# A delta-rule attention layer and its feed-forward layer: the loads for the next unit called at the beginning of a slot

## The chip, the cores and the metric

The kernel runs on one core of a Trainium2 chip. The metric is device time in microseconds (us). Before the change it is 4428.87 us, the median of three runs (4426.77 to 4429.70).

## The reference, cut to what matters

The input x has 4 sequences of 1024 positions with 256 features. The first half is a gated delta-rule attention with 16 key heads and 32 value heads of 128 features each; positions go in chunks of 64. All of it is in 32-bit floats.

```python
mixed = silu(conv4(x @ W_qkv.T))          # causal, 4 taps
q, k, v = split(mixed); q, k = l2n(q), l2n(k)
beta = sigmoid(b);  g = -exp(A_log) * softplus(a + dt_bias);  gc = cumsum(g) in a chunk
decay = exp(gc_i - gc_j) * tril
A  = -((k*beta) @ k.T * decay) * strict
Tm = inverse(eye - A)                     # 64 x 64 for each chunk and head
u  = Tm @ (v*beta);  kcd = Tm @ (k*beta*exp(gc))
# in order of the chunks, with a state S (128 x 128) for each sequence and head:
attn  = (q @ k.T) * decay
v_new = u - kcd @ S
out   = (q*exp(gc)) @ S + attn @ v_new
S     = S * exp(g_last) + (k * exp(g_last - gc)).T @ v_new
y = (out * rsqrt(mean(out**2) + eps) * norm_w * silu(z)) @ W_out.T
```

Then x = x + layernorm(y), and a feed-forward layer (688 inner features, weights taken from a table of 16 values) with a layer norm and a residual of its own.

## The kernel before

**Units, blocks, groups.** The 32 value heads are worked in eight groups of four. A group goes through the 64 chunk positions in 32 tiles of 128 rows: a tile, together with the group's four heads, is a *unit*, so there are 256 units. Within a unit two sequences lie one above the other (64 rows each). Eight units make a *block* (`Super`, 32 in all). The place of a unit in its block, 0 to 7, is u.

**What is made for a unit ahead of its step.** `channel` projects and convolves (matmuls pp, L422; four taps on ACT and DVE, L436 and L439; Silu, L443) and stores q and k in DRAM as qkd (L445). `scores` loads decay rows (dc, L522), multiplies them on POOL (L529 to L536) with the products kkq (L545) and stores the lower triangle lT and the attention scores aT to DRAM (L561). `invert` loads lT for a whole block as lb (L569), inverts all 32 x 32 diagonal pieces at once on DVE by 31 rank-one steps (rank and v, L579 and L580), and stores them as vd (L583). `build` makes the off-diagonal piece of each inverse with two rounds of small matmuls (m1 L611 and m2 L625) out of the loads mt (L599) and pad (L601 and L606), and stores it as nd (L634).

**What the change moves.** `expand(k, u)` (L636 on) lays these out for one unit, with nine DMAs on SP's queue: four ue<-vd (L643) and two ue<-nd (L649) put the inverse pieces at their places in the zeroed tile ue, two ae<-atd (L651) do the same with the scores in ae, and one qku<-qkd (L654) fetches q and k. There are three buffers of ue and of ae, and two of qku.

**The step of a unit.** `step(k, u)` is a generator, and each `yield` ends a part: N0 transposes v into x0; N1 is the product of k and q with the state (pkqs, L683, reads qku); N2 is px (L703, reads ue), the transposes pk (L714, read qku), and the decay of the state on POOL (L720); O3 is po (L703, reads ae) and core (L727). Then J makes squares (L732), and O4 is the state's update (pu, L740, and L747). N parts run in the unit's own slot, O parts in the next one. `project_out` comes five units later (Z, T, U: pz L142, L781 to L785, pto L789, pout L796); it loads the sum ac so far (L775) and stores it again (acc_d, L802).

**The order around the change.** The loop at L871 goes through slots s; slot s runs the step of unit s. A slot's list in `SLOTS` gives the order of the parts by hand, and on TensorE, ScalarE, VectorE and GpSimd instructions stay in that order (`manual_schedule(engines=COMPUTE)`). SP, which issues all DMAs, is not among these: a planner puts its queue in order when the program is built. It takes the transfers that it believes ready, and of several that are ready the one that the program calls for first. On the chip SP then goes through that queue strictly one by one, and waits where a transfer isn't ready yet. The list for the slot that ends in the step of place 7, in which the loads of the next block's place 0 are called for, begins `v1 A b O3 ...`: v1 calls for the lb loads, b for the store of nd. The slot ahead of that one begins with `b`, which calls for the loads mt and pad.

Of the kernel before, what the change touches and what calls it, by code (L numbers as in the profile page):

```python
# [63 lines left out]
def delta_net_ffn_kernel(  # L64
# [243 lines left out]
    with ExitStack() as main:  # L308
# [327 lines left out]
        def expand(k, u):  # L636

            at = (supers.index(k) * SB + u) % NZ
            ue, ae = (zeroed[name][at] for name in ("ue", "ae"))
            for q in range(4):  # L640
                rows = slice(q * BS, (q + 1) * BS)
                src = k.vd[q * BS + u * HG : q * BS + (u + 1) * HG, :, :]
                nc.sync.dma_start(ue[rows, :, rows], src.rearrange("h c i -> c h i"))  # L643
            for ab in range(2):
                a0 = ab * C
                lo, hi = slice(a0, a0 + BS), slice(a0 + BS, a0 + C)
                hb, w = divmod(u * HG, NQ)
                q = slice((2 * ab + hb) * BS, (2 * ab + hb + 1) * BS)
                nc.sync.dma_start(ue[lo, :, hi], k.nd[q, w : w + HG, :])  # L649
                half = slice(a0, a0 + C)  # L650
                nc.sync.dma_start(ae[half, :, half], k.atd[half, u, :, :])  # L651
            k.exp[u] = ue, ae
            qku = sc.tile([P, MG, 2, 2, C], F32, tag="qku", name="qku", bufs=2)
            nc.sync.dma_start(qku.rearrange("p m j a t -> p m j (a t)"), k.qkd[u])  # L654
            k.qku[u] = qku
# [93 lines left out]
        def rms(k, blk):  # L749
            us = slice(4 * blk, 4 * blk + 4)  # L750
            rr = w2.tile([P, 4, HG], F32, tag="rr", name="rr", bufs=3)
            eq = w2.tile([P, 4, MG], F32, tag="eq", name="eq")
            V.tensor_scalar_mul(eq, k.n2[:, us, :, 1], RMS_EPS * D)
            V.scalar_tensor_tensor(
                rr.rearrange("p c (m h) -> p (c m) h", h=2),
                k.ms[:, us, :].rearrange("p c (m h) -> p (c m) h", h=2),
                1.0 / D,
                bc(eq.rearrange("p c m -> p (c m)").unsqueeze(2), [P, 4 * MG, 2]),
                ALU.mult,
                ALU.add,  # L760
            )
            V.reciprocal(rr, rr)
            yield
            A.activation(rr, rr, AF.Sqrt)
            k.rr[blk] = rr
            yield

        def project_out(k, u):

            end = k.last and u == SB - 1 and k.g + 1 < NG  # L770
            wzs = w_z[k.g]
            ti = k.t0 + u
            ac = sc.tile([P, HID], F32, tag="ac", name="ac", bufs=3)
            if k.g:
                nc.sync.dma_start(ac, acc_d[ti])  # L775
            pz = bank("pz")
            by_rows(pz, lambda kc: wzs[:, kc, :], ti)
            if end:
                load_z(k.g + 1)
            zs = t4("zs")  # L780
            A.activation(zs, as4(pz), AF.Silu)  # L781
            yield 1
            G_.tensor_tensor(zs, zs, bc(k.rr[u // 4][:, u % 4, :].unsqueeze(2), h4), ALU.mult)  # L783
            yield 1
            G_.tensor_tensor(zs, zs, k.cores.pop(u), ALU.mult)  # L785
            yield
            pt = bank("pto")
            for h in range(HG):
                T_.transpose(as4(pt)[:, h, :], zs[:, h, :], ident)  # L789
            oT = t4("oT")  # L790
            A.copy(oT, as4(pt))  # L791
            yield
            wo = w_o[k.g]
            pp = bank("pout")
            for h in range(HG):
                T_.matmul(pp[:, :HID], lhsT=oT[:, h, :], rhs=wo[:, h, :], start=h == 0, stop=h == HG - 1)  # L796
            yield 1
            if k.g == 0:
                V.tensor_copy(ac, pp[:, :HID])
            else:  # L800
                V.tensor_add(ac, ac, pp[:, :HID])  # L801
            nc.sync.dma_start(acc_d[ti], ac)  # L802
            if end:
                load_o(k.g + 1)

        def drain(*gens):
            for gen in gens:
                for _ in gen:
                    pass
# [4 lines left out]
        def resume(gen):  # L814
            nonlocal count
            wait = next(gen, None)
            if wait:
                heappush(due, (place + wait, count, gen))
                count += 1

        def go(gen):

            nonlocal place
            late = [entry for entry in due if entry[2] is gen]
            while late:
                due.remove(late[0])
                heapify(due)
                resume(gen)
                late = [entry for entry in due if entry[2] is gen]
            if gen is not None:  # L830
                resume(gen)
            place += 1
            while due and due[0][0] <= place:
                resume(heappop(due)[2])
# [7 lines left out]
        def work(kind, n, *args):  # L842

            if not 0 <= n < len(supers):
                return None
            key = (kind, n, *args)
            if key not in started:
                started[key] = kind(supers[n], *args)
            return started[key]
# [19 lines left out]
        units = [(k, u) for k in supers for u in range(SB)]  # L869
        with tc.manual_schedule(engines=COMPUTE):  # L870
            for s in range(-LQ, len(units)):  # L871
                n, i = divmod(s, SB)
                nq, iq = divmod(s + LQ, SB)
                nv, iv = divmod(s + LV, SB)
                gens = {}
                newer = step(*units[s]) if s >= 0 else None
                for c in "01234":
                    gens["N" + c], gens["O" + c] = newer, older
                gens["J"] = older
                gens["T"] = gens["U"] = gated  # L880
                gated = project_out(*units[s - OUT_LAG]) if s >= OUT_LAG else None
                gens["Z"] = gated
                if 0 <= nv < len(supers):
                    gens["A"] = channel(supers[nv], iv // 4, 2 * MG + iv % 4, 2)
                if nq < len(supers):
                    gens["B"] = channel(supers[nq], iq // 4, iq % 4, 1)
                inv = work(invert, nq - 1 if iq >= 4 else nq - 2)
                made = work(build, nq - 2)

                root = [work(rms, *divmod(s // 4 - 1, 2))] + ([work(roots, n + 1)] if i == 4 else [])  # L890
                for name in SLOTS[iq].split():
                    c = name[0]
                    if c == "v":
                        for _ in range(int(name[1:]) if inv else 0):
                            next(inv, None)
                        continue
                    block = 2 * nq + iq // 4 - (iq % 4 != 2 or c == "s")
                    if c in "rq":
                        for gen in filter(None, root[: 1 if c == "r" else 2]):
                            resume(gen)  # L900
                        continue
                    if c == "n":
                        gen = work(norms, *divmod(block, 2))
                    elif c == "s":
                        gen = work(scores, *divmod(block, 2))
                    elif c == "b":
                        gen = made
                    else:
                        gen = gens.get(name)
                    go(gen)  # L910
                    if name == "O4":
                        next(pieces, None)
                if inv and iq == 2:
                    drain(inv)
                older = newer
                if 0 <= s + 1 < len(units):
                    expand(*units[s + 1])
            drain(older)
            drain(rms(supers[-1], 1))
            drain(*(gen for _, _, gen in sorted(due)))  # L920
            drain(gated)
            for unit in units[len(units) - OUT_LAG :]:
                drain(project_out(*unit))
            drain(pieces)
# [112 lines left out]
```

## Time and profile before

| | |
|---|---|
| median of 3 runs | 4428.87 us |
| the profiled execution | 4427.16 us |
| its span, first to last instruction | 4425.5 us |
| mean granted TensorE clock | 0.971 |
| instructions in the span | 79446 |
| DMA moved | 492.71 MB, 111 GB/s in the mean |

Read from the page: the chain that ended last is 58% TensorE, 24% DVE, 6% ScalarE and 2% DMA. Up to about 280 us the first blocks are prepared, from there to about 4010 us the slots run, about 14.7 us each in the mean, and the feed-forward layer fills the rest. In the rows of DMA issues, the median time from issue to landing is 2.2 us for ue<-vd, 1.9 us for ue<-nd, 2.6 us for ae<-atd and 3.0 us for qku<-qkd. In the groups by line, "out<-in" are the names of the tiles written and read, and "idle before <-releaser" is who ended the wait.

### The profile page before, as it was taken

To read this page: it belongs to the slowest core of one execution; us is meant where nothing else is said; L and a number is where in the kernel's file an instruction comes from. 1 tells how busy PE (TensorE), PEld (TensorE's weight loads), DVE (VectorE), ACT (ScalarE), POOL (GpSimd) and SP (SyncE) were. 2 spreads that over 40 slices of the span, in tenths; PEclk is the share of its full clock that TensorE was granted. 3 is DMA by queue.
4 is the path that set the end of the run, shared out by engine and by line. 5 is a ranking of instruction groups with operands and counts; after the bars stand their busy time and mean duration, and the time that the engine had idled before them with its cause. 6 is when DMAs were issued, how large, how long until landed. Compare 5 with 4: busy or idle time off the path is not lost.

```text
span 4425.5 us, 79446 instructions
## 1 busy us (share of the span) xinstructions
PE 4007.4 (91%) x26664; PEld 2866.6 (65%) x26664; DVE 3510.1 (79%) x6641; ACT 2646.0 (60%) x6573; POOL 2070.6 (47%) x1752
## 2 busy tenths in 40 slices
PE   3679999999999999999999999999999999996888
PEld 2456666676767766666667676676766766673444
DVE  4788888888888898888888888889888888861442
ACT  2456666666666666666666666666666666662111
POOL 2545555655555555554455545555453334332221
PEclk7899999999999999999999999999999999997999
DMA  3444444444444444444444444444444444432110
GB/s 91 118 112 110 111 118 120 127 121 118 126 136 126 119 118 127 119 118 125 130 128 120 117 126 135 125 116 118 123 123 117 123 126 120 101 83 71 37 35 19
DMA packets 1052419, 492.71 MB, mean 111 GB/s; under 512 B 729824, under 2 KB 951152, under 8 KB 1052016
## 3 DMA queue, kind: packets, MB, share of 16 engines
q1 hardware_dynamic: 1052016, 487.64, 41.8%
q8 instruction: 216, 3.54, 0.3%
q14 instruction: 187, 1.53, 0.1%
HBM read 267.66 MB, written 219.69 MB: 110 GB/s over the span
## 4 chain that ended last, share of the span: by engine, by line
PE 58%; DVE 24%; issue 6%; ACT 6%; POOL 3%; DMA 2%; SPq 0%; DVEq 0%; POOLq 0%; ACTq 0%
PE pp L422 13%; DVE cv L439 8%; PE pout L796 7%; PE pz L142 7%; PE pkqs L683 7%; PE px L703 4%; DVE rank L579 4%; PE pu L740 3%; PE po L703 3%; PE pgu L959 3%; PE py L971 2%; PE kkq L545 2%; DVE v L580 2%; PE pto L789 1%; DVE core L727 1%
## 5 line engine op out<-in xcount | busy, mean ns | idle before, releaser
L439 DVE SCALAR_TENSOR_TENSOR cv<-pp,cw,cv 128x512 f32<-128x512 f32 x1536 | 1148.8, 748 | 353.3 <-ACT cv L436 323.7
L783 POOL TENSOR_TENSOR zs<-zs,rr 128x512 f32<-128x512 f32 x256 | 266.4, 1041 | 1578.8 <-ACT zs L781 1569.8
L436 ACT ACTIVATE cv<-pp,cw 128x512 f32<-128x512 f32 x512 | 350.6, 685 | 488.0 <-PE pp L422 487.9
L580 DVE TENSOR_TENSOR v<-v,rank 128x31 f32<-128x31 f32 (+15 forms) x992 | 555.7, 560 | 34.3 <-DVE rank L579 0.3
L422 PE MATMUL pp<-xnT,wq 128*128 128x262 f32 x2048 | 530.1, 401 | 41.9 <-DVE cv L439 32.6
L796 PE MATMUL pout<-wo,oT 128*128 128x256 f32 x2048 | 510.2, 394 | 7.8 <-ACT oT L791 7.8
L422 PEld LDWEIGHTS pp<-xnT,wq 128*128 128x128 f32 x2048 | 372.0, 191 | 214.5 <-issue 56.2
L422 PE MATMUL pp<-xnT,wv 128*128 128x262 f32 x2048 | 503.8, 387 | 5.5 <-DVE cv L439 5.5
L142 PE MATMUL pz<-wzs,xnT 128*64 128x512 f32 x2048 | 488.4, 598 | 4.7 <-DVE ac L801 3.8
L579 DVE TENSOR_TENSOR rank<-v,lb 128x31 f32<-128x31 f32 (+15 forms) x992 | 467.1, 471 | 27.3 <-DMA lb<-ltd 19.6
L683 PE MATMUL pkqs<-S,qku 128*64 128x256 f32 x3840 | 477.5, 387 | 4.7 <-DVE core L727 3.3
L720 POOL TENSOR_TENSOR S<-S,dkm 128x1024 f32<-128x1024 f32 x224 | 436.3, 1948 | 26.6 <-PE pkqs L683 16.1
L703 PE MATMUL px<-x,ue 128*128 128x128 f32 x2048 | 291.9, 286 | 159.5 <-issue 106.9
L703 PEld LDWEIGHTS px<-x,ue 128*128 128x128 f32 x2048 | 263.3, 194 | 260.0 <-issue 150.2
L422 PEld LDWEIGHTS pp<-xnT,wv 128*128 128x128 f32 x2048 | 382.0, 190 | 73.6 <-issue 12.8
L796 PEld LDWEIGHTS pout<-wo,oT 128*128 128x128 f32 x2048 | 386.6, 199 | 55.6 <-ACT oT L791 9.7
L683 PEld LDWEIGHTS pkqs<-S,qku 128*64 128x64 f32 x3840 | 248.7, 136 | 203.0 <-issue 51.0
L732 ACT ACTIVATE junk<-core 128x128 f32<-128x128 f32 x1024 | 318.7, 311 | 66.7 <-DVE core L727 38.4
L785 POOL TENSOR_TENSOR zs<-zs,core 128x512 f32<-128x512 f32 x256 | 328.5, 1283 | 20.1
L708 ACT ACTIVATE xs<-px 128x512 f32<-128x512 f32 x256 | 154.6, 604 | 234.3 <-PE px L703 234.3
L740 PE MATMUL pu<-yg,kt 64*128 64x256 f32 x1920 | 272.2, 402 | 14.2 <-DVE cv L439 13.1
L300 POOL TENSOR_SCALAR lt<-lx,lutb 128x344 f32<-128x344 int32 (+2 forms) x210 | 276.7, 1317 | 16.8
(166 smaller groups left out, 7067.8 us busy)
## 6 DMA issues: line engine op xcount, KB each, us to landing
qkd<-qk SPq DMA_DIRECT2D x256, 256.0 KB, 2.5
qku<-qkd SPq DMA_DIRECT2D x256, 256.0 KB, 3.0
dc<-rows_d SPq DMA_DIRECT2D x256, 128.0 KB, 3.6
ltd<-lT SPq DMA_DIRECT2D x128, 256.0 KB, 2.4
atd<-aT SPq DMA_DIRECT2D x128, 256.0 KB, 2.7
ae<-atd SPq DMA_DIRECT2D x512, 64.0 KB, 2.6
acc_d<-ac SPq DMA_DIRECT2D x256, 128.0 KB, 2.2
ac<-acc_d SPq DMA_DIRECT2D x224, 128.0 KB, 2.5
```

Source lines behind the costliest of these rows:

```text
L142: T_.matmul(ps[ab * C : (ab + 1) * C, :], lhsT=xnT[:, kc, 2 * p + ab, H + n * C : H + (n + 1) * C], rhs=rhs(kc), start=kc == 0, stop=kc == ...
L422: T_.matmul(ps[:, 2 * p : 2 * p + 2, : H + BT], lhsT=wt[:, kc, :], rhs=xnT[:, kc, 2 * p : 2 * p + 2, c0 : c0 + H + BT], start=kc == 0, sto ...
L436: A.activation(cv, ps[:, :, H : H + BT], AF.Copy, scale=cw[:, ch, H : H + 1])
L439: V.scalar_tensor_tensor(cv, ps[:, :, i : i + BT], cw[:, ch, i : i + 1], cv, ALU.mult, ALU.add)
L579: V.tensor_tensor(t, bc(v[:, 0 : j + 1, j : j + 1], sh), bc(lb[:, j : j + 1, j + 1 :], sh), ALU.mult)
L580: V.tensor_tensor(v[:, 0 : j + 1, j + 1 :], v[:, 0 : j + 1, j + 1 :], t, ALU.subtract)
L683: T_.matmul(as4(ps)[ab * C : (ab + 1) * C, two, :], lhsT=qk[:, m, j, ab, :], rhs=S_[:, ab, two, :], start=True, stop=True,)
L703: T_.matmul(as4(ps)[:, h, :], lhsT=w[:, h, :], rhs=src[:, h, :], start=True, stop=True)
L720: G_.tensor_tensor(flat, flat, bc(decay, [P, 2 * HG, P]), ALU.mult)
L740: T_.matmul(as4(pu[:, ab])[:, two, :], lhsT=kt[half, m, :], rhs=yg[half, two, :], start=True, stop=True)
L785: G_.tensor_tensor(zs, zs, k.cores.pop(u), ALU.mult)
L796: T_.matmul(pp[:, :HID], lhsT=oT[:, h, :], rhs=wo[:, h, :], start=h == 0, stop=h == HG - 1)
```

## The change

`expand` for the unit of the next slot was the last thing that a slot did. Now it is called ahead of the slot's list when the next unit is at place 1 to 7 of its block, and right after part O4 when it is at place 0, whose inverse's last piece is stored in that same slot. Nothing that is computed changes, and `expand` itself doesn't.

```diff
                 root = [work(rms, *divmod(s // 4 - 1, 2))] + ([work(roots, n + 1)] if i == 4 else [])
+
+                ahead = units[s + 1] if 0 <= s + 1 < len(units) else None
+                if ahead and ahead[1]:
+                    expand(*ahead)
                 for name in SLOTS[iq].split():
...
                     go(gen)
                     if name == "O4":
                         next(pieces, None)
+                        if ahead and not ahead[1]:
+                            expand(*ahead)
                 if inv and iq == 2:
                     drain(inv)
                 older = newer
-                if 0 <= s + 1 < len(units):
-                    expand(*units[s + 1])
```

## The prediction

> **What bounds the kernel now.** I read the page first, for the bound. (The columns of its first row: busy us, share of the span, number of instructions.)
>
> ```profile
> span 4425.5 us, 79446 instructions
> PE 4007.4 (91%) x26664; PEld 2866.6 (65%) x26664; DVE 3510.1 (79%) x6641; ACT 2646.0 (60%) x6573; POOL 2070.6 (47%) x1752
> PE   3679999999999999999999999999999999996888
> DMA  3444444444444444444444444444444444432110
> ```
>
> From the third slice to about the 36th, TensorE is busy nine tenths of the time or more, and the 16 DMA engines under half of it. The busy times by stretch agree: 948.32 us of TensorE in the 1000 us from 1000 to 2000. What is left of TensorE's idle time between 280 and 4010 us I took from the trace as gaps over 0.4 us: 187 us, of which 157 stand before px (L703), where they end with the last DVE step of x0 (L694). TensorE and DVE bound the loop.
>
> The change moves only DMA issues, so the next question is who waits for the tiles that they fill. Of the answers for the tiles ue (inverses), qku (q and k) and ae (scores), in this order, the part on who waited for it (us, times):
>
> ```profile
> who waited for it (us, times):
>   ACT xs L708: 234.3, 210
>   POOL S L720: 10.6, 1
>   DVE rank L579: 2.0, 2
> ```
> ```profile
>   POOL S L720: 16.1, 2
>   POOL wo L370: 14.8, 3
>   ACT qs L695: 1.7, 3
>   DVE x L694: 1.2, 1
> ```
> ```profile
>   DVE core L727: 75.9, 68
>   DVE lT L555: 1.2, 1
> ```
>
> No row says PE px, pkqs or po: these are waits for matmuls that read the tiles, and three (10.6, 2.0, 1.2 us) that are put down to a load on the same queue while the waiting line does not read it. So I measured each margin in the trace, as the start of a unit's matmul less the landing of its last load. From unit 1 on the smallest is 11.5 us for px after ue, 14.9 us for po after ae and 8.8 us for px after qku (q and k are read first by pkqs, some 6 us before px); the medians are 30.8, 33.0 and 23.1 us. Unit 0 has 4.2 us for ue and still no wait.
>
> Why so early, if the call stands at the end of the slot ahead? The timeline of SP, around slot 118 (its px starts at 2019.89, the po of unit 117, which opens the slot on TensorE, at 2010.63):
>
> ```profile
> 2007.55 0.58 SPq L651 DMA_DIRECT2D ae<-atd  x1
> 2008.23 0.55 SPq L654 DMA_DIRECT2D qku<-qkd  x1
> 2008.88 1.46 SPq L522 DMA_DIRECT2D dc<-rows_d  x1
> ...
> 2021.28 0.33 SPq L569 DMA_DIRECT2D lb<-ltd  x1
> 2024.10 0.33 SPq L802 DMA_DIRECT2D acc_d<-ac  x1
> 2025.11 0.37 SPq L445 DMA_DIRECT2D qkd<-qk  x1
> 2025.53 1.81 SPq L569 DMA_DIRECT2D lb<-ltd  x3
> 2027.57 1.11 SPq L634 DMA_DIRECT2D nd<-nb  x1
> 2028.72 1.39 SPq L643 DMA_DIRECT2D ue<-vd  x3
> ```
>
> The first two rows are the last loads of unit 119, which slot 118 calls for at its end: they are out before slot 118 begins. SP is not among the engines whose order is written by hand. Its queue stands in an order that the planner chose when it believed each transfer ready, and the place of the call is only a rank among transfers that are ready together. I counted this over the run: all nine loads of unit s+1 are issued before the px of unit s in every slot that I counted (units 16 to 239), and for places 2 to 7 in a block of eight mostly (57 to 100% by place) before slot s has begun. For places 0 and 1 (the place of a unit in its block of eight) they reach into the slot.
>
> **The change, part by part.** Removed: 256 calls at the end of a slot. Added: the same calls, 224 of them ahead of the slot's list and 32 (for a unit at place 0 of its block) after its O4. No compute instruction is added or moved, and their order stays. Each call issues nine transfers, 2304 in all: four ue<-vd, two ue<-nd, two ae<-atd, one qku<-qkd. By the medians of their rows one call holds SP for 4 x 0.430 + 2 x 0.432 + 2 x 0.586 + 0.433 = 4.19 us, before and after. So the sum on the path is: added work 0; stall removed from TensorE 0, since it never waited for these loads.
>
> What can move is the transfers of the same slot that were issued ahead of an expand and are now ranked behind it, by at most 4.19 us each. I took their cover from landing to first reader:
> - ac<-acc_d (L775): at least 21.8 us until L801. In 26 of the 28 blocks that have it, it stands ahead of all loads of the units at places 0 and 1; now it may come after those of place 1. Cost 0.
> - dc<-rows_d (L522): at least 8.3 us until the POOL step L529. In the slot that calls for place 4's loads it now ranks behind them. 8.3 - 4.2 leaves 4.1 us. Cost 0; if that cover were gone, POOL, at 47%, would be late with the scores.
> - pad<-vd from L606: at least 9.4 us until the matmuls L625; mt<-ltd: at least 61 us. Both are issued by build in the slot that calls for place 7's loads, and rank behind these now. Cost 0.
> - pad<-vd from L601: only 0.24 to 3.8 us until the matmuls L611, most often about 3. But it waits for a store of this same slot (L593, issued at 2012.48 once ACT's copy is done), and the loads of unit 119 are out at 2008.8 already. Cost 0.
> - lb<-ltd (L569): the tight one. The inversion's first step L579 waits for it on DVE:
>
> ```profile
>   DMA lb<-ltd: 19.6, 16
> ```
> One of these waits, 6.6 us, is at the start; the other 15 make 13.0 us. In the rows above lb stands ahead of unit 120's loads, and the call for place 0, even after O4, stays behind lb in program order (lb is called for at the first step of the same slot). Cost 0.
>
> A call made earlier might also put a waiting transfer at SP's head. The largest row of SP's own waits says how much of that there is already:
>
> ```profile
> SPq L643 <- PE pk L714: 507.0, 102, 8.1
> ```
> Here SP stands at a first ue<-vd until an older unit's matmuls have let its buffer go, up to 8.1 us, with everything else queued behind. The Trainium skill ("Perfetto Trace Analysis", DMA Instruction — HWDGE) has the semaphore wait on the issuing sequencer, ahead of the descriptors, since the DMA engines themselves don't wait. That speaks against an earlier call: by the rule, a slot whose expand stands first could hold its stores and loads for up to 8.1 us more. The row shows that these waits come from the planner's idea of when the buffer is free, since they exist although the call stands at the slot's end. The buffers are three for ue and ae and two for qku, and are let go one to two slots ahead of either place, so neither place makes a new wait. By the rule, with 32 lb loads held 8.1 us, the sum is up to +259 us; by the row it is 0. I take 0, as all nine loads precede px of the slot today. The opposite rule ("DMA: Bandwidth & Descriptors", Rules for kernel authors: issue the DMA early, wait on its semaphore late) would promise a gain; with 8.8 us of smallest margin there is nothing to collect.
>
> The lower bound of the unknown: a regrouped queue may happen to send the three last lb loads ahead of the qkd store that they now follow (2025.11 above), and that could remove at most the 13.0 us of DVE waits. The upper bound is priced in the slower rival.
>
> **The rivals.**
> *Forecast, no change that can be measured:* the queue's order changes within its slack. Profiled execution 4427.16 us (span 4425.5 and 1.7 around it) + 0 = 4427.2; the median of the runs shown stands 1.7 us above that, so 4429 us, with 5 us either side for a fraction of a microsecond here and there in 32 blocks. Chance 0.72.
>
> *Faster:* lb passes the store, the 13.0 us of DVE waits go, and DVE is what TensorE's px waits for. Against it: the largest of these waits does not reach TensorE. With 1.63 us of it (at 594 us) the eight slots from px of unit 15 to unit 23 take 598.94 - 477.75 = 121.19 us; in the same phase of the next group without such a wait (units 47 to 55) 1077.19 - 955.90 = 121.29. It would need the full 13 us, and gives 4416; a part gives 4420 and less is in the forecast. Chance 0.11.
>
> *Slower:* the regrouped nine loads fall in front of the lb loads (or of the ltd store that they read) at the turn of a block, 32 times. Price: up to 4.19 us each, less the 1.6 us of lateness that the comparison above shows to be free. So it decides from 1.6 us on, about four loads put in front; all nine cost 4.19 - 1.6 = 2.6 us x 32 = 83 us (4512), and six of them 6 x 0.47 - 1.6 = 1.2 us x 32 = 38 us (4467). The rows above speak against it: lb is ranked ahead of place 0's loads, and place 7's are long out. For it speaks only that lb's own margin is nil. Chance 0.17, most of it near the low end.
>
> That the change doesn't do what it says is in effect the forecast: the place of the call doesn't set the time of the issue.
>
> **How the numbers follow.** About 0.2%, 8.9 us, is what a measurement of this kernel can tell from no change. Same 0.72, faster 0.11, slower 0.17, as the cases. The forecast's own range is 4424 to 4434; with 8 in 10 wanted it is reached to the faster case's nearer part and the slower one's low end: 4419 to 4441. The predicted time is the forecast's, 4429.
>
> **What would show it.** Right, if the order of TensorE, DVE, ACT and POOL is as before, px still has ue some 30 us ahead in the median, and in the timeline of SP the loads of a unit stand closer together, with dc and ac behind them. L775 and L522 should then land later at no cost, and the row lb<-ltd stay near 19.6 us in total. Wrong, if a row "PE px <- DMA ue" or "PE m <- DMA pad" appears, if the lb row grows past some 50 us (32 x 1.6), or if the 507.0 us of SP's waits at L643 grow and the qkd or ltd stores behind them come late.

## The result: no change that can be measured

| | before | after |
|---|---|---|
| median of 12 runs each | 4431.07 us | 4433.44 us |
| ratio, 95% interval | | 1.0005 (0.9996 to 1.0014) |
| the same measured once more (e1_again) | 4430.23 us | 4429.42 us |
| ratio, 95% interval | | 1.0001 (0.9993 to 1.0009) |
| span of the profiled execution | 4425.5 us | 4432.7 us, and 4425.9 us in e1_again |

Both intervals hold 1 and end inside the 0.2% that the prediction named. The two profiled spans of the same changed kernel, 4432.7 and 4425.9 us, show how much of a single span's difference is the execution's own. It is not waiting: between the first px of the first unit and that of the last, TensorE is idle for 201.4 us in the one and 200.8 in the other, against 202.6 before the change. It is the granted clock: 0.968 in the mean in the one and 0.970 in the other, with 4021.3 and 4009.9 us of TensorE's busy time for the same matmuls (the last section says where the clock is lost). The prediction was 4429 us, 4419 to 4441.

The page of the changed kernel, first its span, busy times and the 40 slices of TensorE:

```profile
span 4432.7 us, 79363 instructions
PE 4021.3 (91%) x26664; PEld 2876.3 (65%) x26664; DVE 3514.5 (79%) x6641; ACT 2646.0 (60%) x6573; POOL 2069.1 (47%) x1752
PE   3679999999999999999999999999999999995888
```

On TensorE, DVE, ACT and POOL the counts of instructions are those of before, and instruction by instruction none has another place in its engine's order. On SP 1649 of 4478 transfers have. Counted in places of the queue, 425 of the 1024 ue<-vd come earlier (up to 16 places), as do 271 of the 512 ue<-nd, 321 of the 512 ae<-atd and 120 of the 256 qku<-qkd. For that 190 of the 224 ac<-acc_d come later (up to 24 places, 7.4 in the mean over all), and 120 of the 256 dc<-rows_d. None of the 128 lb loads has another place. So the change did something, and a good deal of it. SP's timeline at the stretch that was shown of before:

```profile
2007.06 0.41 SPq L654 DMA_DIRECT2D qku<-qkd  x1
2007.52 0.45 SPq L606 DMA_DIRECT2D pad<-vd  x1
2008.01 0.48 SPq L775 DMA_DIRECT2D ac<-acc_d  x1
2008.59 1.22 SPq L522 DMA_DIRECT2D dc<-rows_d  x1
...
2012.88 1.22 SPq L643 DMA_DIRECT2D ue<-vd  x2
...
2020.78 0.33 SPq L569 DMA_DIRECT2D lb<-ltd  x1
2023.60 0.33 SPq L802 DMA_DIRECT2D acc_d<-ac  x1
2024.61 0.37 SPq L445 DMA_DIRECT2D qkd<-qk  x1
2025.03 1.81 SPq L569 DMA_DIRECT2D lb<-ltd  x3
2027.07 0.66 SPq L634 DMA_DIRECT2D nd<-nb  x1
2027.77 0.93 SPq L643 DMA_DIRECT2D ue<-vd  x2
```

Unit 119's last two loads stood behind the last pad load. Now both stand ahead of it: qku is out at 2007.06 in place of 2008.23, ae at 2001.05 in place of 2007.55. The tight part, from lb to nd, is in the same order to the row, and only the ue loads behind it have lost one of three to an earlier place. That place is ahead of lb: the two at 2012.88 are unit 120's. One of them stood there before the change too, in a row of before that the prediction's timeline does not show:

```profile
2014.26 0.47 SPq L643 DMA_DIRECT2D ue<-vd  x1
```

Who waits for ue, and what DVE's inversion waits for, in the tile views of ue and lb:

```profile
who waited for it (us, times):
  ACT xs L708: 237.4, 212
```
```profile
  DMA lb<-ltd: 18.8, 17
```

The row for ue is the only one: still no TensorE among its waiters. For lb there are 18.8 us where there were 19.6. Of SP's own waits the first row:

```profile
SPq L643 <- PE pk L714: 512.6, 101, 8.3
```

That is 507.0 us of before with 5.6 added. Summed over the four lines of `expand` and all releasers, SP's waits grew more, from 711.9 to 776.9 us (773.7 in e1_again): the earlier call does hold SP a little longer, by 0.25 us for each unit, and all of SP's waits together went from 2129 to 2159 us. TensorE's idle time, above, did not grow with it.

### The profile page after: what moved, and what is told of

The parts are those of the page before. It is cut to its first block, busy times and chain, and to the rows that moved or that the text cites. A ratio compares the mean times of both kernels' runs of the same rounds, so it can differ in the third digit from the quotient of the medians.

```text
span 4432.7 us, 79363 instructions
## 1 busy us (share of the span) xinstructions
PE 4021.3 (91%) x26664; PEld 2876.3 (65%) x26664; DVE 3514.5 (79%) x6641; ACT 2646.0 (60%) x6573; POOL 2069.1 (47%) x1752
## 4 chain that ended last, share of the span: by engine, by line
PE 59%; DVE 24%; issue 6%; ACT 6%; POOL 3%; DMA 2%; SPq 1%; DVEq 0%; POOLq 0%; ACTq 0%
PE pp L422 13%; DVE cv L439 8%; PE pout L796 7%; PE pz L142 7%; PE pkqs L683 7%; PE px L703 4%; DVE rank L579 4%; PE pu L740 4%; PE po L703 3%; PE pgu L963 3%; PE py L975 2%; DVE v L580 2%; PE kkq L545 2%; PE pto L789 2%; PE pv L670 1%
## 5 line engine op out<-in xcount | busy, mean ns | idle before, releaser
L579 DVE TENSOR_TENSOR rank<-v,lb 128x31 f32<-128x31 f32 (+15 forms) x992 | 468.2, 472 | 24.5 <-DMA lb<-ltd 18.8
L703 PE MATMUL px<-x,ue 128*128 128x128 f32 x2048 | 296.1, 289 | 157.5 <-issue 102.2
L683 PEld LDWEIGHTS pkqs<-S,qku 128*64 128x64 f32 x3840 | 249.2, 136 | 201.4 <-issue 51.0
L740 PE MATMUL pu<-yg,kt 64*128 64x256 f32 x1920 | 272.2, 402 | 15.4 <-DVE cv L439 14.0
```

The costliest lines, as they stand in the source:

```text
L579: V.tensor_tensor(t, bc(v[:, 0 : j + 1, j : j + 1], sh), bc(lb[:, j : j + 1, j + 1 :], sh), ALU.mult)
L683: T_.matmul(as4(ps)[ab * C : (ab + 1) * C, two, :], lhsT=qk[:, m, j, ab, :], rhs=S_[:, ab, two, :], start=True, stop=True,)
L703: T_.matmul(as4(ps)[:, h, :], lhsT=w[:, h, :], rhs=src[:, h, :], start=True, stop=True)
L740: T_.matmul(as4(pu[:, ab])[:, two, :], lhsT=kt[half, m, :], rhs=yg[half, two, :], start=True, stop=True)
```

## The experiments

Every ratio is to the kernel before, run on the same chip beside it. The margins are computed from each trace like those of the prediction, but for the units 8 to 247 alone: a unit's matmul start less the landing of its last load.

**The change once more (e1_again).** No edit.

> The change once more, to narrow the interval. The theory (the call's place is only a rank among transfers that are ready together, and every transfer that changes places has slack) expects a ratio to the kernel before of 0.998 to 1.002. The rival (the small loss of the first measurement is real, from dc or lb loads that now come later) expects 1.001 to 1.003 with an interval that leaves out 1, and more idle time of DVE's rank before lb<-ltd than 19.6 us.

Measured: 1.0001 (0.9993 to 1.0009). With the first measurement this leaves at most about 0.1% either way. The rival's second sign is there by its letter: DVE's waits for lb are 21.4 us in this execution. But 7.6 us of that are one wait at the start. After 280 us they are 13.8 us here, 11.4 in the first execution of the changed kernel and 13.0 before: no trend, and the rival of a small real loss is not supported.

**The call moved the other way (e2_after_n0).**

```diff
-            qk, vt = k.qku.pop(u), k.vt[blk]
+            vt = k.vt[blk]
...
             yield
+            qk = k.qku.pop(u)
             if not first:
...
+                    if name == "N0" and 0 <= s < len(units):
+                        expand(*units[s])
...
-                if 0 <= s + 1 < len(units):
-                    expand(*units[s + 1])
```

> The call moved the other way: for a unit's own loads, in its own slot, right behind its first part N0, so one part ahead of the first reader pkqs. The theory expects the same time (ratio 0.998 to 1.002), as the planner issues the loads when their buffers are free, about 26 us ahead of the reader, wherever the call stands; the median margin of px after ue stays over 25 us. The rival (the place of the call sets the time of the issue) expects nine issues of 4.2 us and a landing of 3.0 us in front of each pkqs, of which N0 covers some 3 us: about 4 us in each of 256 slots, 1000 us in all, 5400 us.

Measured: 4432.32 us, 1.0004 (0.9996 to 1.0012). A call that stands one part ahead of the first reader is as good as one that stands a slot ahead. The median margin of px after ue is 31.1 us (31.0 before, 31.6 after the change), qku lands 15.4 us ahead of its first reader pkqs (16.6 before), and 178 transfers of SP's queue change places. The place of the call does not set the time of the issue; the rival's 1000 us are out.

**The planner taken away (e3_sp_hand_end, e4_sp_hand_start).** Both add SP to the engines whose queue stays in program order; e3 to the kernel before, e4 to the changed one.

```diff
     mybir.EngineType.Pool,
+    mybir.EngineType.SP,
 }
```

> The kernel before, with SP among the engines whose queue stays in program order, so that no planner moves a transfer. If the planner is what makes the call's place harmless, the loads now go out at the slot's end, behind the slot's last stores, and land some 7 us into the next slot, where pkqs is due after about 3 us: 4 us in each of 256 slots, about 1000 us, 5000 to 5600 us in all, with waits of PE for qku or ue. The rival (the loads are hidden whatever the order) expects less than 4550 us.

> The changed kernel, with SP's queue in program order too. The theory expects that the early call now does what it says: the loads go out a slot ahead, px, pkqs and po do not wait for them, and the kernel is 500 to 1300 us faster than the one with the call at the slot's end in the same order, though slower than the kernel before by whatever else program order costs (4450 to 4900 us). The rival (loads hidden whatever the order) expects the two to lie within 1% of each other.

Measured: e3 6197.18 us, 1.3989 (1.3970 to 1.4008); e4 4767.88 us, 1.0766 (1.0749 to 1.0782). In this order the very edit that does nothing in the kernel under study is worth 6197 - 4768 = 1429 us. e4 lies in its range; e3 is beyond its 5600, and the difference beyond the 1300 that was expected at most. In e3's rows of waits (us in total, times, longest us) the largest on PE and the largest of SP:

```profile
PE pkqs L684 <- DMA qku<-qkd: 1432.0, 228, 11.3
```
```profile
SPq L446 <- ACT qk L444: 1787.0, 226, 18.7
```

SP stands at a store of q or k until ACT has made it, and in this order the next unit's loads stand behind. TensorE then has 228 waits of 6.3 us each, where I had put 4 us. One of them, from the timeline of the same kernel:

```profile
3003.61 0.55 SPq L655 DMA_DIRECT2D qku<-qkd  x1
...
3006.94 3.68 PE L684 MATMUL pkqs<-S,qku 128*64 128x256 f32 x16 [9.38 <-DMA qku<-qkd]
```

TensorE stands still for 9.38 us and starts 3.3 us after the load's issue, which is the load's own landing. Beside that the clock fell: TensorE's busy time for the same instructions is 4476.4 us in place of 4007.4, and the mean granted clock 0.842 in place of 0.971. I had not reckoned with that; the last section shows where it falls.

With the call at the slot's beginning (e4) that wait is gone: in e4's tile view of qku no PE pkqs stands among the waiters, and pkqs starts 8.4 us after qku's landing in the median. What e4 still loses to the kernel before, 338 us, is elsewhere, since program order holds up other transfers too. Its rows of waits, and SP's row of before for comparison:

```profile
PE m L612 <- DMA pad<-vd: 193.0, 32, 10.2
```
```profile
SPq L446 <- ACT qk L444: 1125.4, 214, 18.5
```
```profile
SPq L445 <- ACT qk L443: 185.8, 124, 9.3
```

SP still stands at the stores of q and k, 1125 us in all against 185.8 before. TensorE waits 193 us for pad loads, where the planned order has one such wait of 5.9 us, and its busy time is 106 us longer (4113.3 us).

**The price of a late lb (e5_lb_behind9, e6_lb_behind4).** With 9, or 4, in the place of N; the added tile is read by nobody.

```diff
             lb = sc.tile([P, BS, BS], F32, tag="lb", name="lb")
+            more = sc.tile([P, N, BS], F32, tag="more", name="more")
+            for j in range(N):
+                nc.sync.dma_start(more[:BS, j, :], k.ltd[:BS, SB - 1 - j % 2, j % HG, :BS])
```

> The kernel before, with nine more loads (32 x 32 floats each, of the last rows of the stored lower triangle, into a tile that nobody reads) called for just ahead of the four lb loads of each block: the price of the slower rival, by itself. The last lb should land about 3.5 us later. By the prediction's price (1.6 us free, the rest paid 32 times) 60 us slower, 4490 us; without a free part 110 us, 4540 us; if DVE has room for all of it, less than 9 us.

> The same with four more loads, which puts the last lb about 1.2 us later. By the prediction's price it is free (ratio 0.998 to 1.002); without a free part it costs 38 us, 4469 us.

Measured: e5 4499.57 us, 1.0154 (1.0140 to 1.0168); e6 4441.18 us, 1.0016 (1.0009 to 1.0022). The tile view of lb, what DVE's idle time before it ended with, in e5 and then in e6:

```profile
  DMA lb<-ltd: 150.3, 32
```
```profile
  DMA lb<-ltd: 70.7, 32
```

In e5 the last lb lands 4.2 us later than before (13.0 us after the lower triangle's last store in place of 8.8, medians), in e6 1.7 us later (10.5). From the ratios e5 costs 0.0154 x 4432 = 68 us, 2.1 us in each of 32 blocks, and e6 0.0016 x 4432 = 7 us, 0.2 us a block. So some 1.5 to 2 us are nearly free, and what comes beyond is paid, as the prediction's 1.6 us had it. Where the cost lies can be seen in the traces. Between the px of the first and of the last unit, TensorE's idle time is 202.6 us before, 200.6 in e6 and 249.1 in e5. So the 7 us of e6 are not idle time. They go with the clock, whose mean over the executions is 0.9677 in e6 and 0.9694 in the kernel before, run beside it: 0.0017 x 4432 = 7.5 us. Whether the later lb is what lowers the clock was not separated. In e5 46.5 us are idle time there, by the one profiled execution; the mean clock over its executions is lower too (0.9645).

**lb made early (e9_lb_first, e10_lb_first_start).** The loads get a rank ahead of everything else; e9 on the kernel before, e10 on the changed one.

```diff
+                with tc.high_priority():
-                nc.sync.dma_start(lb[rows, :, :], k.ltd[...])
+                    nc.sync.dma_start(lb[rows, :, :], k.ltd[...])
```

> The kernel before with the four lb loads of a block ranked ahead of all else, so that they go out together and no longer stand behind a store: the gain of the faster rival, by itself. The last lb should land about 4 us earlier (8.8 us after the lower triangle's store at present, then about 4.8), and the idle time of rank before it after 280 us, 15 us, should be nearly gone. If these waits reach the end (the rival), 10 to 15 us faster, ratio 0.9967. If the first 1.6 us of lateness are free, as the prediction has it, and as four more loads in front of lb cost only 0.16%, ratio 0.999 to 1.001.

> The same on the changed kernel (calls at the slot's beginning). By the theory the two do not help each other: ratio to the kernel before as for the one without the change, 0.999 to 1.001. By the rival that the early call pushes something urgent behind it (which the rank of lb would now repair), this one is 0.1% or more faster than the changed kernel alone.

Measured: e9 4430.35 us, 0.9999 (0.9991 to 1.0007); e10 4434.77 us, 1.0008 (1.0000 to 1.0016). The wait is nearly gone in e9 (7.1 us, of which 5.5 are the one at the start):

```profile
  DMA lb<-ltd: 7.1, 6
```

The last lb lands 2.6 us earlier (6.2 us after the store; I had expected 4), and the end does not move. So these waits of DVE did not reach it: the faster rival's mechanism is out, and not only its chance of being triggered. e10 is not faster than the changed kernel alone either. Neither version beats the kernel before.

**The buffers cut, not the call moved (e7_two_buffers, e8_one_qku).** e7 makes both edits, e8 the second alone.

```diff
-        NZ = 3
+        NZ = 2
...
-            qku = sc.tile([P, MG, 2, 2, C], F32, tag="qku", name="qku", bufs=2)
+            qku = sc.tile([P, MG, 2, 2, C], F32, tag="qku", name="qku", bufs=1)
```

> The kernel before with the buffers cut, not the call moved: two of ue and ae in place of three, one of qku in place of two. The theory says that the free buffer sets the issue, so the loads must come about a slot (14.7 us) later: median margin of px after ue near 16 us in place of 30.8, after qku near 8 in place of 23.1, and some waits at places 0 and 1 of a block, 10 to 60 us in all. The rival (buffers play no part, the queue is full anyway) expects unchanged margins and an unchanged time.

> Of the cut buffers only that of q and k: one of qku, three of ue and ae. The theory expects the margin of ue to stay near 30 us and that of qku to fall to about 8 us before px, that is about 2 us before its first reader pkqs, so that most of the cost of the cut comes from here: 10 to 50 us. If the cost comes from ue or ae in place of it, this one is within 0.2% of the kernel before.

Measured: e7 4445.88 us, 1.0029 (1.0019 to 1.0040); e8 4437.35 us, 1.0017 (1.0008 to 1.0025). The margins come down as forecast. px after ue: 16.6 us in e7 and 31.1 in e8, against 31.0; px after qku: 8.9 and 9.6 against 23.2. Now there is a row that neither kernel of the study has, in e7's waits and then in e8's:

```profile
PE pkqs L683 <- DMA qku<-qkd: 17.6, 24, 2.0
```
```profile
PE pkqs L683 <- DMA qku<-qkd: 14.1, 12, 3.1
```

e8's 0.0017 x 4432 = 7.5 us is a little under the 10 to 50 that I had put, and over half of e7's 13 us. It also lies within the 0.2% that would have spoken for ue and ae, so the time alone doesn't tell where e7's cost comes from; the new row and the margins show that qku now comes too late in some units. What e7 loses besides cannot be given to ue and ae alone, for its queue was regrouped so that lb lands 2.2 us later too (11.0 us after the store), and e6 shows that 1.7 us of that cost 7 us. That share was not separated. What the pair shows is that one buffer fewer moves the loads by a slot, where the call's move by nearly a slot moved their median by 0.6 us.

## Why the prediction was right, point by point

- *The number:* 4429 against 4433.44 us measured. Of the 4.4 us between them, 2.2 are the kernel before, which took 4431.07 us in the twelve runs and 4428.87 in the three that were shown.
- *The loads are not waited for, and moving them removes nothing:* right. The margin of px after ue was 31.0 us in the median and is 31.6, and the rows of waiters have no PE in either kernel, but for a single weight load of pkqs put down to qku for 0.3 us after the change, in which qku lands 7.0 us or more ahead of every pkqs of units 8 to 247.
- *The place of the call is only a rank, and the buffer that comes free sets the issue:* this was argued from SP's order in the trace; e2 (later call, same time), e7 and e8 (fewer buffers, margins down by a slot) and e3 against e4 (no planner, 1429 us between the two places) show it.
- *What is pushed behind has slack:* right. ac<-acc_d had at least 21.8 us until its reader and has 18.1; the first reader of dc had at least 8.3 us from 400 us on and has 8.0, and of the four pairs of dc loads in a block the third fell from 26.6 to 20.9 us in the median; the pad loads of L606 went from 9.4 to 8.7 at least. Of waits for a DMA, TensorE's px has three rows in the changed kernel that it had not before (dkm 2.5, dc 1.4 and ac 1.4 us, one wait each), but it reads none of these, and the same three units (66, 122 and 154) stood still for 2.5, 1.5 and 1.4 us before, put down to "issue" in the first and to ACT in the others: the name of the releaser changed, not the wait. All idle time of TensorE before px sums to 159.5 us before and to 157.5 after. The pad loads of L601 keep their 0.24 us in the tightest place.
- *lb keeps its place:* right, for all 128 loads, but not for the reason given. The prediction had all of place 0's loads behind lb because they are called for behind it. In 18 of the 31 turns of a block one of the nine was ahead of lb already, and now two are, as in the timeline above; in five more turns it was three or four, and is four. Here too the planner did not keep to the order of the calls. It cost nothing, as other transfers moved behind lb in their place: the last lb lands 8.8 us after the lower triangle's last store before, and 8.7 after (medians after 280 us).
- *The faster rival* (up to 13 us if lb passes the store): it was not triggered, and e9 shows that it would have given nothing.
- *The slower rival* (lb pushed back, paid from 1.6 us on): not triggered either, as lb lands no later. Its price was near the truth, 68 us for 4.2 us of lateness where I had 83, and 0.2 us per block for 1.7 us where I had 0.1.
- *The rule that a wait sits on the issuing sequencer:* it says what an order costs, not that the order changes. SP's wait at L643 went from 507.0 to 512.6 us and that at all of `expand`'s lines by 65 us, and the time did not move, where the rule alone would have put up to 259 us. "Neither place makes a new wait" was a little too strong for SP itself. In e3 and e4, with program order, SP's waits are what makes the loads late (1787.0 and 1125.4 us at one line).

## What to carry to other kernels

Before a load is called for earlier, look at who waits for its tile, and at how long ahead of its reader it lands; if it lands two slots ahead, there is nothing to win. Then ask what decides when it is issued. Where a planner orders the queue, as here, that was the moment at which source and buffer were believed ready: one buffer fewer moved the loads by a slot, and the call's place only broke ties. Where the queue stood in program order, the call's place was worth 1429 us. And a wait of an engine is worth what its removal brings to the end, which an experiment on that one wait tells: 13 us of DVE's waits here were worth nothing, while 4 us more of the same in each block cost 68. Compare TensorE's idle time and its granted clock apart, as either can move the end.

## What the runs showed of the hardware that I had not expected

A wait of TensorE can cost more than its own length. In e3 (busy 72% of the span in place of 91%) the same 26664 matmuls kept TensorE busy for 4476.4 us in place of 4007.4, and the mean granted clock was 0.842 in place of 0.971. The loss is not spread over all matmuls. The matmuls of pkqs, the first product behind the wait, in the tile views of qku before and in e3 (ns: least, median, most):

```profile
L683 PE MATMUL pkqs<-S,qku x3840: 379/379/431, 278.8 to 4006.2; 128*64 128x256 f32 x192
```
```profile
L684 PE MATMUL pkqs<-S,qku x3840: 378/634/691, 296.1 to 5784.3; 128*64 128x256 f32 x192
```

The other groups keep their usual medians (px 275 ns in both, po 275, pp 382). About the wait that ends at 3006.94, the trace has the granted clock at 0.50 from 3001.0 to 3011.2, so in the wait and over the matmuls right behind it, and at 1.00 on both sides.

How long must the wait be? From unit 8 on, of TensorE's waits of over 4 us all 186 in e3 and all 31 in e4 were followed by such slow matmuls (three or more within 9 us that took over 1.4 times their median of before). In the kernel before, none of 36 waits of 1 to 2 us was, 3 of 18 of 2 to 2.5 us, and 11 of 22 of 2.5 us to the longest, 3.1. So the kernel under study sits where a wait before px may or may not cost clock. From px of unit 1 to that of the last unit it has 16 stretches at half the clock, 52.1 us in all; the two executions of the changed kernel have 20 and 18 (68.3 and 59.1 us), e3 has 229 (1740.8 us). That is one source of the spread between executions of the same kernel: of the 34 runs of the kernel before beside e5 to e8, the fastest (4427.62 us) had a mean clock of 0.972 and the slowest (4441.40 us) of 0.967. In e4, busy 86%, the clock was 0.943 and the busy time 4113.3 us. In e3 the waits for q and k, 1432 us, are therefore not the whole of the 1767 us that it lost; some 469 us are longer busy time, and some 152 us of idle time before px fell away (159.5 us before, 7.8 in e3).
